# A recommender kernel: an empty GpSimd instruction between row gathers, and the schedule rebuilt around it

## The chip, the cores and the metric

The kernel runs on one core of one Trainium2 chip. A core has five engines [...]: TensorE (PE in the profile, with its weight loads shown apart as PEld), VectorE (DVE), ScalarE (ACT), GpSimd (POOL) and SyncE (SP). Sixteen DMA engines move data between the large memory and the on-chip memory.

The metric is device time in microseconds (us), the median of several executions. These executions are timed without the profiler. The profile is taken of one more execution of the same program, with the profiler on. For this kernel the two differ a lot, and the difference matters for all that follows.

## The reference, cut to what matters

For each of 16384 rows of the batch, the reference averages 32 rows of a table of 50000 x 300 numbers, averages 20 rows from each of three small tables, takes one row from each of four more, and sends the joined 748 features through three layers. A "wide" term, a sum of one number per index, is added before the sigmoid.

```
tok = word_emb[token_idx].mean(axis=1)          # 32 rows of 300
e1 = emb_mh1[mh1_idx].mean(axis=1)              # 20 rows of 64, table of 1000
e2 = emb_mh2[mh2_idx].mean(axis=1)              # ... 5000
e3 = emb_mh3[mh3_idx].mean(axis=1)              # ... 10000
o1..o4 = emb_oh1[oh1_idx], ...                  # one row of 64 each
emb = concatenate([tok, e1, e2, e3, o1, o2, o3, o4], axis=1)    # 748 wide
wide = wide_mh1[mh1_idx].sum(...) + ... + wide_oh4[oh4_idx]
h = relu(emb @ W1 + b1)                         # 748 -> 1024
h = relu(h @ W2 + b2)                           # 1024 -> 512
h = relu(h @ W3 + b3)                           # 512 -> 256
return sigmoid(h @ Wd + bd + wide)              # 256 -> 1
```

All of it is in float32.

## The kernel before

The batch is worked on in 128 tiles of 128 rows. For every tile there are four streams of work.

1. The token rows. GpSimd issues 32 indirect DMAs for a tile; each fetches one row of 300 floats into each of the 128 partitions. Two gathers fill one buffer (a group), there are 6 buffers, and VectorE adds the rows up three groups later. This is 4096 gathers in all.

```
TOK_GROUP = 2
TOK_LAG = 3
tokp = ctx.enter_context(tc.tile_pool(name="tok", bufs=2 * TOK_LAG))

def add_up(t, q, rows):
    a, b = rows[:, 0:TOK_D], rows[:, TOK_D : 2 * TOK_D]
    if q == 0:
        nc.vector.tensor_add(tok_sum, a, b)
    else:
        nc.vector.tensor_add(tok_sum, tok_sum, a)
        to = features[t][:, 0:TOK_D] if q == n_groups - 1 else tok_sum
        nc.vector.tensor_add(to, tok_sum, b)

def tokens(t, it):
    for q in range(n_groups):
        rows = tokp.tile([P, TOK_GROUP * TOK_D], F32, name="tok_rows")
        for r in range(TOK_GROUP):
            j = q * TOK_GROUP + r
            nc.gpsimd.indirect_dma_start(
                out=rows[:, r * TOK_D : (r + 1) * TOK_D],
                out_offset=None,
                in_=word,
                in_offset=bass.IndirectOffsetOnAxis(ap=it[:, j : j + 1], axis=0),
            )
        under_way.append((t, q, rows))
        if len(under_way) > TOK_LAG:
            add_up(*under_way.pop(0))
        yield 1
```

2. The small tables. They stay on chip, each number split into three bf16 parts (`terms`). VectorE makes one-hot rows, TensorE multiplies pairs of them to counts (`pc`), ScalarE writes the counts as fp8 (`cnt`), and in the next tile TensorE multiplies the counts by the tables (`pg`, 138 matmuls for a tile). A tile is cut into 11 steps (`STEPS`), and one step makes the counts of 6 rows in each half of the tile.

3. The layers. Four tiles make a block of 512 rows. Its features are transposed by TensorE, chunk by chunk, and go through the layers as float32 matmuls that are 512 wide. These matmuls are woven between the steps of the next block's tiles.

```
def transposed(x, gs):
    n = len(gs) * P
    for k in range(NK):
        kk = chunk_k[k]
        pt = ps_h.tile([P, BLOCK], F32, name="pt", tag="ph")
        for s, g in enumerate(gs):
            nc.tensor.transpose(pt[:kk, s * P : (s + 1) * P], chunk(g, k), ident)
        nc.vector.tensor_scalar(
            x[:kk, k, 0:n], pt[:kk, 0:n], scale[:kk, k : k + 1], None, ALU.mult
        )
        yield CHUNK_WORK
# ... layer(): for each of n_out outputs, one matmul for each input chunk, then a Relu on ScalarE
```

4. The conversion of the tables to `terms`, once, at the start. VectorE takes the remainders after each bf16 part.

```
for c in range(3):
    ...
    if c:
        nc.vector.scalar_tensor_tensor(
            rows, rows, 2.0 if c == 1 else 1.0, term[c - 1], op0=ALU.mult, op1=ALU.subtract
        )
    nc.scalar.activation(term[c], rows, AF.Copy, scale=2.0 if c == 0 else 1.0)
```

The order in which the instructions of a step are written is the order in which each engine runs them (the schedule is manual). In one step these follow each other: the next one-hots, the counts, one piece of the table conversion, the share of the tile's token groups, the share of the sums over the small tables, and the share of the layers.

```
for i in range(STEPS):
    ...
    hot = one_hots(sc, s, i + 1)
    counts(cnt, hot_now, i)
    tables_on_chip.to(TABLE_PACE * (t * STEPS + i - 2))
    toks.to(n_groups * (i + 1) / STEPS)
    done = next(sums) if sums else 0
    if layers:
        share = (n_h + layers_time) * (i + 1) / STEPS - done
        layers.to((layers_before + share) / LAYER_TIME)
```

Of the kernel before, what the change touches and what calls it, by code (L numbers as in the profile page):

```python
# [17 lines left out]
P = 128  # L18
# [5 lines left out]
TOK_LAG = 3  # L24
BLOCK = 512
HALF = P // 2
N_SMALL = 3 * N_MH + 4
ONEHOT = 6
STEPS = -(-HALF // ONEHOT)
CHUNK_WORK = 1  # L30
TABLE_PACE = 1.2
LAYER_TIME = 10
# [6 lines left out]
G_COLS = TOK_D + 7 * ROW  # L39
# [7 lines left out]
def kernel(  # L47
# [23 lines left out]
    NSUB = BLOCK // P  # L71
# [5 lines left out]
    for f in SMALL:  # L77
# [4 lines left out]
    tokp = ctx.enter_context(tc.tile_pool(name="tok", bufs=2 * TOK_LAG))  # L82
    const = ctx.enter_context(tc.tile_pool(name="const", bufs=1))
    idxp = ctx.enter_context(tc.tile_pool(name="idx", bufs=2))
# [4 lines left out]
    gp = ctx.enter_context(tc.tile_pool(name="g", bufs=NSUB + 1))  # L89
    wp = ctx.enter_context(tc.tile_pool(name="wide", bufs=2 * NSUB))  # L90
    xp = ctx.enter_context(tc.tile_pool(name="x", bufs=1))
# [8 lines left out]
        [(0, 128)],  # L100
        [(128, 256)],
        [(256, 300), (684, 748)],
        [(300, 428)],
        [(428, 556)],
        [(556, 684)],
    ]
# [7 lines left out]
    scale = const.tile([P, NK], F32, name="scale")  # L114
    nc.vector.memset(scale, 1.0)
    nc.vector.memset(scale[:, 0:2], 1.0 / N_TOK)
    nc.vector.memset(scale[0 : TOK_D - 256, 2:3], 1.0 / N_TOK)
    nc.vector.memset(scale[:, 3:4], 1.0 / N_MH)
    nc.vector.memset(scale[0:EMB, 4:5], 1.0 / N_MH)
# [23 lines left out]
    PART = n_h // 6  # L143

    def load_tables(part0, tag):
        raw = xp.tile([P, PART, ROW], F32, name="raw", tag=tag)
# [14 lines left out]
    def convert_tables():  # L161


        tags = ("even", "odd")
        raws = [load_tables(k * PART, tags[k]) for k in range(2)]
        yield
        for part in range(n_h // PART):
            rows = raws[part]
            if 1 <= part < n_h // PART - 1:
                raws.append(load_tables((part + 1) * PART, tags[(part + 1) % 2]))  # L170
            for c in range(3):
                term = [
                    terms[:, part * PART : (part + 1) * PART, k * ROW : (k + 1) * ROW]
                    for k in range(3)
                ]
                if c:
                    nc.vector.scalar_tensor_tensor(
                        rows, rows, 2.0 if c == 1 else 1.0, term[c - 1], op0=ALU.mult, op1=ALU.subtract
                    )
                nc.scalar.activation(term[c], rows, AF.Copy, scale=2.0 if c == 0 else 1.0)  # L180
                yield 1
# [22 lines left out]
    under_way = []  # L204
    features = {}

    def add_up(t, q, rows):

        a, b = rows[:, 0:TOK_D], rows[:, TOK_D : 2 * TOK_D]
        if q == 0:  # L210
            nc.vector.tensor_add(tok_sum, a, b)  # L211
        else:
            nc.vector.tensor_add(tok_sum, tok_sum, a)  # L213
            to = features[t][:, 0:TOK_D] if q == n_groups - 1 else tok_sum
            nc.vector.tensor_add(to, tok_sum, b)  # L215

    def tokens(t, it):


        for q in range(n_groups):  # L220
            rows = tokp.tile([P, TOK_GROUP * TOK_D], F32, name="tok_rows")
            for r in range(TOK_GROUP):
                j = q * TOK_GROUP + r
                nc.gpsimd.indirect_dma_start(  # L224
                    out=rows[:, r * TOK_D : (r + 1) * TOK_D],
                    out_offset=None,
                    in_=word,
                    in_offset=bass.IndirectOffsetOnAxis(ap=it[:, j : j + 1], axis=0),
                )
            under_way.append((t, q, rows))  # L230
            if len(under_way) > TOK_LAG:
                add_up(*under_way.pop(0))
            yield 1

    def last_tokens():
        for group in under_way:
            add_up(*group)

    def load_indices(blk):
# [15 lines left out]
        return it, ix  # L255
# [71 lines left out]
    def small_sums(g, cnt):  # L327
# [3 lines left out]
        for i in (0, 2, 4, 6):  # L331
# [9 lines left out]
            at = TOK_D + i * ROW  # L341
# [9 lines left out]
    def wide_term(g):  # L351
        wide = wp.tile([P, 1], F32, name="wide")
        at = TOK_D + EMB
        nc.vector.tensor_reduce(
            wide,
            g[:, at : at + 6 * ROW].rearrange("p (c d) -> p c d", d=2 * ROW)[:, :, 0:2],
# [3 lines left out]
        nc.vector.tensor_add(wide, wide, g[:, G_COLS - 1 : G_COLS])  # L360
        return wide

    def chunk(g, k):
        if k < 2:
            return g[:, k * P : (k + 1) * P]
        if k == 2:
            return g[:, 2 * P : TOK_D + EMB]
        at = TOK_D + (1 + 2 * (k - 3)) * ROW + 1
        return g[:, at : at + 2 * EMB]

    def transposed(x, gs):

        n = len(gs) * P
        for k in range(NK):
            kk = chunk_k[k]
            pt = ps_h.tile([P, BLOCK], F32, name="pt", tag="ph")
            for s, g in enumerate(gs):
                nc.tensor.transpose(pt[:kk, s * P : (s + 1) * P], chunk(g, k), ident)  # L378
            nc.vector.tensor_scalar(  # L379
                x[:kk, k, 0:n], pt[:kk, 0:n], scale[:kk, k : k + 1], None, ALU.mult  # L380
            )
            yield CHUNK_WORK

    def layer(dst, weights, bias, src, kks, n_out, n):
# [180 lines left out]
```

## Time and profile before

| | us |
|---|---|
| timed executions, without the profiler | 7128.85, 7092.46, 7119.63 |
| their median | 7119.63 |
| the profiled execution | 5271.1 |
| its span in the trace | 5269.3 |

The profiled execution is 1848.5 us shorter than the median of the timed ones. The views of the profile show the profiled execution only.

| engine, profiled execution | busy us | share of the span | instructions |
|---|---|---|---|
| PE | 5094.7 | 97% | 41320 |
| DVE | 3768.8 | 72% | 8014 |
| ACT | 2447.1 | 46% | 1938 |
| POOL | 3897.3 | 74% | 4103 |

How to read the views: a group is a set of instructions of one source line, with its engine, what it writes and reads, the count behind the x, the busy time in us and the mean of one in ns, and after the second bar the idle time of the engine just before these instructions with the name of what ended most of the wait. "issue" means that the engine waited for nothing that the profile shows. In a timeline the columns are the start and the duration in us, the engine, the line, the operation, and in square brackets the idle time before it with its releaser. The ends of matmuls are modelled, so PE's share is not a share of its peak.

### The profile page before, as it was taken

How to read it: one execution, taken by the hardware profiler on the slowest of the kernel's cores; microseconds unless marked ns; L12 is line 12 of the kernel's file. 1: busy time of each engine (PE TensorE's matmuls, PEld its weight loads, DVE VectorE, ACT ScalarE, POOL GpSimd, SP SyncE). 2: the span in 40 equal slices, each digit the busy share in tenths (PEclk: the TensorE clock that was granted, in tenths of full speed). 3: DMA queues.
4: the chain of work that ended last, by engine and by line, in shares of the span. 5: the costliest groups of instructions: out<-in, count | busy, mean ns of one | idle time of the engine just before them, and what ended most of it. 6: DMA issues, size and time to landing. Idle time of an engine off the chain costs nothing.

```text
span 5269.3 us, 104252 instructions
## 1 busy us (share of the span) xinstructions
PE 5094.7 (97%) x41320; PEld 3164.7 (60%) x41320; DVE 3768.8 (72%) x8014; ACT 2447.1 (46%) x1938; POOL 3897.3 (74%) x4103
## 2 busy tenths in 40 slices
PE   4799999999999999999999999999999999999999
PEld 3565656566565656656655656556566566656658
DVE  8777777777777777777777777777777777777752
ACT  5444444444444444444444444444444444444432
POOL 7777777777777777777777777777777777777762
PEclk8899999999999999999999999999999999999999
DMA  6444444444444444444444444444444444444431
GB/s 190 125 125 124 125 125 126 126 125 124 125 125 125 125 124 125 125 125 126 125 124 125 126 125 126 124 125 125 125 125 125 124 126 125 125 125 125 124 103 34
DMA packets 252890, 652.60 MB, mean 124 GB/s; under 512 B 119009, under 2 KB 119524, under 8 KB 252399
## 3 DMA queue, kind: packets, MB, share of 16 engines
q0 software_dynamic: 196608, 629.41, 43.5%
q1 hardware_dynamic: 55791, 16.53, 1.4%
q8 instruction: 323, 5.29, 0.4%
q14 instruction: 168, 1.38, 0.1%
HBM read 645.59 MB, written 0.07 MB: 123 GB/s over the span
## 4 chain that ended last, share of the span: by engine, by line
PE 37%; DMA 23%; DVE 16%; issue 14%; POOL 10%; ACT 0%; DVEq 0%; SPq 0%; POOLq 0%; ACTq 0%
DMA tok_rows<-in_word_emb_dram,it 22%; PE ph L388 20%; PE pg L337 12%; POOL tok_rows L224 10%; DVE own L215 5%; PE pc L312 4%; DVE own L213 3%; DVE slice L294 3%; DVE row L294 2%; DVE x L379 1%; DVE g L343 1%; PE po L413 1%; DVE own L211 0%; DVE g L215 0%; PE po L417 0%
## 5 line engine op out<-in xcount | busy, mean ns | idle before, releaser
L224 POOL DMA_INDIRECT tok_rows<-in_word_emb_dram,it x4096 | 3896.4, 951 | 1293.4 <-issue 755.5
L319 ACT ACTIVATE cnt<-pc 128x1656 fp8e3<-128x1656 f32 (+1 forms) x1408 | 2121.7, 1507 | 2056.4 <-PE pc L312 2026.0
L337 PE MATMUL pg<-terms,cnt 128*128 128x195 bf16 x17664 | 1849.6, 254 | 87.7 <-DVE g L343 86.3
L337 PEld LDWEIGHTS <-cnt 128*128 128x128 fp8e3 x17664 | 1601.3, 144 | 234.6 <-issue 81.1
L388 PE MATMUL ph<-x,w_sb 128*128 128x512 f32 (+5 forms) x3264 | 1474.1, 581 | 4.2 <-DVE x L379 3.5
L215 DVE TENSOR_TENSOR own<-own,tok_rows 128x300 f32<-128x300 f32 x1792 | 857.7, 479 | 680.6 <-DMA tok_rows<-in_word_emb_dram,it 647.3
L388 PE MATMUL ph<-h,w_sb 128*128 128x512 f32 (+2 forms) x2720 | 1211.0, 573 | 0.0
L213 DVE TENSOR_TENSOR own<-own,tok_rows 128x300 f32<-128x300 f32 x1920 | 918.8, 479 | 387.6 <-DMA tok_rows<-in_word_emb_dram,it 335.8
L312 PEld LDWEIGHTS <-row 64*128 64x128 bf16 x16384 | 501.7, 95 | 1041.3 <-DVE own L215 246.1
L294 DVE TENSOR_TENSOR row<-own,sc 128x768 bf16<-128x768 bf16 (+1 forms) x1408 | 762.4, 541 | 162.8 <-PE pc L312 89.5
L312 PE MATMUL pc<-slice,row 64*128 64x138 bf16 x16384 | 758.4, 224 | 70.6 <-DVE slice L294 36.7
L388 PEld LDWEIGHTS ph<-x,w_sb 128*128 128x128 f32 (+1 forms) x3264 | 564.3, 194 | 414.6 <-issue 401.9
L294 DVE TENSOR_TENSOR slice<-own,sc 128x828 bf16<-128x828 bf16 (+1 forms) x1408 | 797.9, 567 | 0.0
L388 PEld LDWEIGHTS ph<-h,w_sb 128*128 128x128 f32 x2720 | 463.3, 192 | 317.9 <-issue 316.0
L397 ACT ACTIVATE h<-ph,b_sb 128x512 f32<-128x512 f32 (+2 forms) x476 | 316.3, 665 | 683.2 <-PE ph L388 678.2
L343 DVE TENSOR_REDUCE g<-pg 128x130 f32<-128x390 f32 (+1 forms) x512 | 259.2, 506 | 151.1 <-PE pg L337 150.8
L379 DVE TENSOR_SCALAR x<-pt,scale 128x512 f32<-128x512 f32 (+4 forms) x204 | 137.0, 712 | 3.7 <-PE pt L378 2.9
L378 PE MATMUL pt<-ident,g 128*128 128x128 f32 (+1 forms) x768 | 104.1, 275 | 3.0 <-DVE x L379 2.5
L211 DVE TENSOR_TENSOR own<-tok_rows 128x300 f32<-128x300 f32 x128 | 61.4, 480 | 49.5 <-DMA tok_rows<-in_word_emb_dram,it 47.3
L378 PEld LDWEIGHTS pt<-ident,g 128*128 128x128 f32 (+1 forms) x768 | 85.5, 141 | 7.7 <-DVE x L379 6.7
L215 DVE TENSOR_TENSOR g<-own,tok_rows 128x300 f32<-128x300 f32 x128 | 60.2, 471 | 22.3 <-DMA tok_rows<-in_word_emb_dram,it 18.3
L413 PE MATMUL po<-h,wd_sb 128*1 128x512 f32 (+2 forms) x136 | 60.9, 566 | 0.3
(34 smaller groups left out, 290.1 us busy)
## 6 DMA issues: line engine op xcount, KB each, us to landing
tok_rows<-in_word_emb_dram,it POOLq DMA_INDIRECT x4096
ix<-in_idx_dram SPq DMA_DIRECT2D x128, 32.0 KB
w_sb<-in_W_dram SPq DMA_DIRECT2D x6, 512.0 KB
raw<-in_mh_dram SPq DMA_DIRECT2D x3, 747.5 KB
it<-in_idx_dram SPq DMA_DIRECT2D x32, 64.0 KB
w_sb<-in_W_dram SPq DMA_DIRECT2D x1, 2048.0 KB
raw<-in_mh_dram SPq DMA_DIRECT2D x1, 617.5 KB
out_dram<-h SPq DMA_DIRECT2D x31, 2.0 KB
```

The lines of the kernel that those rows point to most:

```text
L213: nc.vector.tensor_add(tok_sum, tok_sum, a)
L215: nc.vector.tensor_add(to, tok_sum, b)
L224: nc.gpsimd.indirect_dma_start(out=rows[:, r * TOK_D : (r + 1) * TOK_D], out_offset=None, in_=word, in_offset=bass.IndirectOffsetOnAxis(ap ...
L294: nc.vector.tensor_tensor(one[:, 0:rows, :].rearrange("p i (n d) -> p i n d", d=2), iota[:, 0:n].rearrange("p (n d) -> p n d", d=2).unsque ...
L312: nc.tensor.matmul(pc[:, f, k // n, at : at + n_h], hot[0][half, k, :], hot[1][half, k, :], start=True, stop=True,)
L319: nc.scalar.activation(cnt[:, :, b : b + rows, :].rearrange("l f (g k) h -> l f g (k h)", g=2), pc[:, :, :, 0 : n * n_h], AF.Copy, scale=0 ...
L337: nc.tensor.matmul(pg[:, j, :], by_slice[:, :, h], terms[:, h, :], start=(h == h0), stop=(h == h1 - 1))
L343: nc.vector.tensor_reduce(g[:, at : at + n * ROW].rearrange("p (f d) -> p f d", f=n), pg[:, 0:n, :].rearrange("p f (c d) -> p f d c", c=3) ...
L378: nc.tensor.transpose(pt[:kk, s * P : (s + 1) * P], chunk(g, k), ident)
L379: nc.vector.tensor_scalar(x[:kk, k, 0:n], pt[:kk, 0:n], scale[:kk, k : k + 1], None, ALU.mult)
L388: nc.tensor.matmul(ph[:, 0:n], weights[:kk, k, m * P : (m + 1) * P], src[:kk, k, 0:n], start=(k == 0), stop=(k == len(kks) - 1),)
L397: nc.scalar.activation(dst[:, m, 0:n], ph[:, 0:n], AF.Relu, bias=bias[:, m : m + 1])
```

## The change

The change has these parts.

- An empty GpSimd instruction, `engine_nop`, follows every gather. It computes nothing and nobody waits for it.
- The token groups are no longer tied to their tile. One generator runs over all 1024 groups, and is paced over 704 + 16 steps (`WAKE`), so that the gathers drift behind the counts by up to 16 steps. There are 8 buffers in place of 6, and the sums of a tile's tokens get a tile of their own (`g_tok`).
- The transposes are made tile by tile, the small tables' features and the tokens' apart, each as soon as it is there. The order of the chunks is changed so that the small features come first. The wide term is a 65th column that is transposed along, and is added by VectorE behind the last layer, in place of a matmul for each tile.
- A block of the layers is two tiles (256 rows) in place of four.
- The remainders of the table conversion are made by TensorE, in PSUM: the identity times the rows, minus one half times the terms so far. VectorE has no part in it any more. The pieces are smaller (7 of the 138 slices at once in place of 23).

It is meant to let the gathers follow each other faster, and to keep the other engines from waiting for one another once they do.

```diff
+TOK_BUFS = 8
+WAKE = 16
+LAYER_TILES = 2
+SPLIT = 7
+PART = 3 * SPLIT
-LAYER_TIME = 10
+LAYER_TIME = 2.5
...
-    def tokens(t, it):
-        for q in range(n_groups):
-            rows = tokp.tile([P, TOK_GROUP * TOK_D], F32, name="tok_rows")
-            for r in range(TOK_GROUP):
...
+    def tokens():
+        under_way = []
+        for n in range(n_all):
+            if n < n_all - TOK_LAG:
+                t, q = divmod(n, n_groups)
+                it = token_indices[t // NSUB][:, t % NSUB, :].bitcast(U32)
+                rows = tokp.tile([P, TOK_GROUP * TOK_D], F32, name="tok_rows")
+                for r in range(TOK_GROUP):
+                    j = q * TOK_GROUP + r
+                    nc.gpsimd.indirect_dma_start(
+                        out=rows[:, r * TOK_D : (r + 1) * TOK_D],
+                        out_offset=None,
+                        in_=word,
+                        in_offset=bass.IndirectOffsetOnAxis(ap=it[:, j : j + 1], axis=0),
+                    )
+                    nc.gpsimd.engine_nop()
+                under_way.append((t, q, rows))
+            if n >= TOK_LAG:
                 add_up(*under_way.pop(0))
             yield 1
...
-                if c:
-                    nc.vector.scalar_tensor_tensor(
-                        rows, rows, 2.0 if c == 1 else 1.0, term[c - 1], op0=ALU.mult, op1=ALU.subtract
-                    )
-                nc.scalar.activation(term[c], rows, AF.Copy, scale=2.0 if c == 0 else 1.0)
...
+            left = ps_h.tile([P, SPLIT, ROW], F32, name="left", tag="ph")[:, 0 : b - a, :]
+            nc.tensor.matmul(left, ident, rows(p), start=True, stop=False)
+            for k in range(c):
+                nc.tensor.matmul(left, minus_half, term(p, k), start=False, stop=(k == c - 1))
+            nc.scalar.activation(term(p, c), left, AF.Copy, scale=2.0)
...
+        def add_small(self, t, g):
+            at = self.columns(t)
+            pt = ps_h.tile([P, 4, P], F32, name="pt", tag="ph")
+            nc.tensor.transpose(pt[:, 3, :], g[:, 0:P], ident)
+            for k in range(3):
+                c = (1 + 2 * k) * ROW + 1
+                nc.tensor.transpose(pt[:, k, :], g[:, c : c + P], ident)
+            ...                                        # scaled copies to x_small, one row to wide_row
+        def add_tokens(self, t, g):
+            ...                                        # three transposes, scaled copies to x_tok, x_small
...
+    n_steps = tiles * STEPS + WAKE
...
+        if waiting and step >= waiting[0][0]:
+            block = transpose(*waiting.pop(0)[1:])
+            if block:
+                if layers:
+                    layers.finish()
+                layers = Paced(mlp(block), LAYER_TIME * block.n / P)
+                ...
+        toks.to(n_all * (step + 1) / n_steps)
...
         if layers:
-            layers_before += layers_time
...
+            layers.to(mlp_work * layers.size * (step + 1 - begin) / left + ahead)
```

## The prediction

> **What bounds the kernel now.** I read the times first, then the page's table of engines, the timeline of GpSimd at the start, the groups, and the timeline of TensorE near the end, where the last blocks are narrower.
>
> The times disagree with the trace: 7119.63 us as the median of the timed executions, 5271.1 us for the profiled one. The trace therefore shows the kernel's work, but not what makes it last 7120 us. The first question is which engine can hide 1848 us.
>
> ```profile
> PE 5094.7 (97%) x41320; PEld 3164.7 (60%) x41320; DVE 3768.8 (72%) x8014; ACT 2447.1 (46%) x1938; POOL 3897.3 (74%) x4103
> ...
> L224 POOL DMA_INDIRECT tok_rows<-in_word_emb_dram,it x4096 | 3896.4, 951 | 1293.4 <-issue 755.5
> ...
> L215 DVE TENSOR_TENSOR own<-own,tok_rows 128x300 f32<-128x300 f32 x1792 | 857.7, 479 | 680.6 <-DMA tok_rows<-in_word_emb_dram,it 647.3
> ...
> L213 DVE TENSOR_TENSOR own<-own,tok_rows 128x300 f32<-128x300 f32 x1920 | 918.8, 479 | 387.6 <-DMA tok_rows<-in_word_emb_dram,it 335.8
> ```
>
> PE looks like the bound, but its share is of modelled ends. VectorE's largest waits are for the gathers' transfers (647 and 336 us), and GpSimd itself waits mostly for "issue", that is for nothing. The timeline of GpSimd shows this from the first gather on, before the other engines have anything to hold it back with:
>
> ```profile
> 3.12 1.10 POOL L224 DMA_INDIRECT tok_rows<-in_word_emb_dram,it  x1 [1.65 <-DMA it<-in_idx_dram]
> 4.53 0.95 POOL L224 DMA_INDIRECT tok_rows<-in_word_emb_dram,it  x1 [0.30 <-issue]
> 5.78 0.95 POOL L224 DMA_INDIRECT tok_rows<-in_word_emb_dram,it  x1 [0.30 <-issue]
> 7.04 0.95 POOL L224 DMA_INDIRECT tok_rows<-in_word_emb_dram,it  x1 [0.30 <-issue]
> ...
> 22.07 1.50 POOL L224 DMA_INDIRECT tok_rows<-in_word_emb_dram,it  x1 [0.30 <-issue]
> ...
> 25.16 2.09 POOL L224 DMA_INDIRECT tok_rows<-in_word_emb_dram,it  x1 [0.30 <-issue]
> ...
> 5190.39 0.94 POOL L224 DMA_INDIRECT tok_rows<-in_word_emb_dram,it  x1 [0.30 <-issue]
> ```
>
> The reader is to see the start-to-start distance: 1.253 us, with 0.95 us in the gather and 0.30 us behind it. Over the whole timeline 4039 of the 4095 distances lie between 1.2 and 1.3 us. So 4096 x 1.253 = 5132 us, out of the 5187 us from the first gather to the last. The missing 57 us are the few longer distances: 43 of them after 5000 us, where the buffers come free late, and 11 in the first 130 us. Behind the last gather come 79 us of tail. The profiled execution is bound by GpSimd, one gather after the other.
>
> PE is a close second. I worked out its floor from distances in the same trace[...].
>
> ```profile
> 5134.80 0.54 PE L312 MATMUL pc<-slice,row 64*128 64x138 bf16 x12
> 5135.27 0.39 PE L337 MATMUL pg<-terms,cnt 128*128 128x195 bf16 x2
> 5135.50 4.48 PE L388 MATMUL ph<-h,w_sb 128*128 128x512 f32 x10
> 5139.91 0.42 PE L312 MATMUL pc<-slice,row 64*128 64x138 bf16 x8
> ...
> 5198.06 4.51 PE L388 MATMUL ph<-h,w_sb 128*128 128x256 f32 x20
> 5202.50 0.42 PE L312 MATMUL pc<-slice,row 64*128 64x138 bf16 x8
> ```
>
> Ten passes of 512 columns take 4.41 us (5135.50 to 5139.91), twenty passes of 256 take 4.44 us. Twelve count matmuls take 0.47 us, and fifteen small-table matmuls 1.36 us (5112.95 to 5114.31 in the same view). A block of four tiles has 180 layer passes, since float32 is recorded as two. For a tile: counts 128 x 0.04 = 5.1; small tables 138 x 0.0907 = 12.5; layers 180 x 0.441 / 4 = 19.8; transposes and the wide term about 1.0. That is 38.4 us, and 128 tiles make 4920 us, 4% below the gathers' 5132.
>
> For the timed executions nothing else has room for 1848 us. PE would have to be slower by more than a third, against a granted clock of 0.989 in the trace. If the gathers set the pace there as well, one takes (7119.6 - 79) / 4096 = 1.72 us, 0.47 us more than under the profiler. This is an inference: no view shows a timed execution.
>
> [...] the DMA engines are busy only four tenths of the time. [...] the gathers of 1.50 and 2.09 us above coincide with the table remainders (1.72 us at 21.03 and 1.71 us at 24.72). [...]
>
> **The change, part by part.**
>
> The empty instruction: 4096 of them on GpSimd. [...] the change puts something between them without the profiler. I take it that this has the same effect, and that a gather with its empty instruction then takes what it takes in the trace, 1.253 us. Removed from the path: 4096 x (1.72 - 1.253) = 1913 us. If the empty instruction added 0.05 us behind each gather, 205 us would come back; I see 0.30 us of pause already in each distance and count nothing.
>
> The drift is a hint of the same number. The gathers are spread over 720 steps and the counts over 704. That only makes sense where the gathers are slower by about 2% than the rest. With the rest at 4920 us plus 1 to 2% of stalls, the gathers would be near 5100 to 5150, and 5132 fits.
>
> More buffers and the drift: the 57 us of long distances shrink, mostly the 43 at the end. VectorE's adds in program order no longer wait as often. I count 40 us gained.
>
> Layers in blocks of two: 180 passes of 0.222 for two tiles make 20.0 us for a tile in place of 19.8, 17 us in all on PE, and PE has slack. The extra Relu instructions go to ScalarE, which is busy 46%.
>
> Transposes tile by tile: seven for a tile in place of six, but no more wide matmuls (256 in all); even on PE. On VectorE five smaller copies for a tile replace six of 0.74 us for four tiles; some 1.5 us more for a tile, 200 us on an engine with 1500 us idle, off the path.
>
> Tables by TensorE: 12 VectorE instructions of 1.71 us go, and with them some 10 us of delayed gathers in the first 130 us. The PE has room there.
>
> The tail: behind the last gather there remain the landing and the adds (about 4 us), the transposes and copies (about 2), one tile's layers of 180 passes of 0.11 us (96 passes take 10.8 us at the end of the trace, so 20 us), the sigmoid and the store (about 3): near 30 us in place of 79.
>
> Sum: first gather at 3, 4096 gathers at 1.253 = 5132, long distances 20, tail 30: 5185 us. I add 15 us for the uncertain cost of the empty instruction and predict 5200 us, a saving of 1920 us or 27%.
>
> **The rivals.**
>
> First: the empty instruction does nothing, and a gather stays at 1.72 us. For it: no view shows the cause of the 0.47 us, and if the profiler speeds up the gathers by something else (another path of dispatch, a slower neighbour), an instruction more is only a cost. Then the rest of the change brings the tail, 50 us, and loses up to 200: 7070 to 7320 us. Against it: the whole rest of the change only pays once the gathers are quick.
>
> Second: the gathers become quicker than in the trace[...]. Then PE is the bound: 4920, plus about 90 us at the start while there is nothing for the layers to do yet, plus 20 of tail and 1% of stalls: about 5080 us. For it: the 0.30 us pause has no cause in the trace.
>
> Third: the empty instruction works in part or has a price, 1.3 to 1.4 us for a gather: 5375 to 5785 us.
>
> Fourth: the time before has to do with PE's clock outside the profile, not with gathers. Then the change, which leaves PE's work as it is, would leave 7100 us. The granted clock speaks against it.
>
> **Range and chances.** I give the main path about 60%, the second rival 15, the third 13, and the two without a gain 12. The main path and the second rival span 5050 to 5290; part of the third has to be in the range. So 5050 to 5480. Faster by over 2% in 0.88, within 2% in 0.06, slower in 0.06.
>
> **What would show the steps right or wrong.** The timed executions should come to within 3% of the profiled one. In the trace of the changed kernel GpSimd's distances should stay at 1.25 us or a little more, from 3 us to about 5160 us, with hardly a long one, and the rest behind the last gather should be near 30 us. PE's pairs at 256 columns should be 0.222 us apart. If the timed executions stay above 7000 us while the trace shows 5200, the step "the empty instruction does what the profiler does" is wrong; if the trace shows distances above 1.4 us, its price is wrong; if PE runs without a gap and GpSimd waits for VectorE, the second rival is right.

## Result: slower by 7.5%

| | before | after |
|---|---|---|
| median of the timed executions, us | 7120.24 | 7651.85 |
| lowest to highest | 7092.46 to 7128.85 | 7636.04 to 7655.15 |
| ratio after/before | | 1.0749, 95% interval 1.0716 to 1.0783 |
| span of the profiled execution, us | 5269.3 | 7633.9 |
| its mean granted TensorE clock | 0.989 | 0.874 |

Predicted were 5200 us, in a range of 5050 to 5480. The changed kernel's profiled execution is as long as its timed ones. That makes the 5269 us trace of the kernel before, on which the prediction stood, the one to be doubted; experiment 1 tests it.

### The profile after

The page of the changed kernel: engines with busy time and share, the granted clock in 40 slices (tenths of full speed), the chain that ended last, and the groups.

```profile
PE 5989.8 (78%) x46912; PEld 4706.2 (62%) x46912; DVE 3890.9 (51%) x8502; ACT 2577.7 (34%) x2445; POOL 3878.3 (51%) x4103
...
PEclk8888888888888898888898988888888888888889
...
PE 52%; another core or an unknown queue 19%; DVE 13%; issue 11%; ACT 5%; DVEq 0%; SPq 0%; DMA 0%; ACTq 0%
...
L255 POOL DMA_INDIRECT tok_rows<-in_word_emb_dram,it x4096 | 3877.4, 947 | 3715.7 <-DVE own L242 2425.8
L348 ACT ACTIVATE cnt<-pc 128x1656 fp8e3<-128x1656 f32 (+1 forms) x1408 | 2123.8, 1508 | 3203.6 <-remote 1658.8
L366 PE MATMUL pg<-terms,cnt 128*128 128x195 bf16 x17664 | 2179.9, 273 | 428.2 <-issue 380.1
...
L323 DVE TENSOR_TENSOR row<-own,sc 128x768 bf16<-128x768 bf16 (+1 forms) x1408 | 763.0, 542 | 1848.7 <-remote 1374.1
```

No engine is the bound: PE falls from 97% to 78%. GpSimd's gathers are as short as before (947 ns against 951), but it now waits 2426 us for VectorE to free a buffer. VectorE and ScalarE in turn wait for "remote", and 19% of the chain is "another core or an unknown queue". There is one core only. The words mean that the view found no instruction whose end lies close before the end of the wait. Both waiting instructions, the counts' copy and the next one-hots, wait for TensorE's count matmuls.

The timeline of GpSimd answers to the one shown of the kernel before (start, duration, engine, instruction, idle time before it with its releaser):

```profile
3.09 1.10 POOL L255 DMA_INDIRECT tok_rows<-in_word_emb_dram,it  x1 [1.62 <-DMA it<-in_idx_dram]
4.49 0.95 POOL L255 DMA_INDIRECT tok_rows<-in_word_emb_dram,it  x1 [0.30 <-issue]
...
24.61 0.95 POOL L255 DMA_INDIRECT tok_rows<-in_word_emb_dram,it  x1 [0.30 <-issue]
25.86 0.94 POOL L255 DMA_INDIRECT tok_rows<-in_word_emb_dram,it  x1 [0.30 <-issue]
27.11 0.95 POOL L255 DMA_INDIRECT tok_rows<-in_word_emb_dram,it  x1 [0.30 <-issue]
33.66 0.94 POOL L255 DMA_INDIRECT tok_rows<-in_word_emb_dram,it  x1 [5.61 <-DVE own L242]
...
7593.56 0.94 POOL L255 DMA_INDIRECT tok_rows<-in_word_emb_dram,it  x1 [0.30 <-issue]
```

The distance is 1.25 us with the 0.30 us pause, as before, and the two stretched gathers near 22 and 25 us are gone. 81% of all distances are still below 1.3 us. What makes the time is the others, such as the 5.61 us at 33.66.

What happens in such a wait, in the timeline of all engines in the middle of the changed kernel:

```profile
2988.50 1.48 PE L443 MATMUL ph<-h,w_sb 128*128 128x256 f32 x6
...
2993.59 0.54 PE L341 MATMUL pc<-slice,row 64*128 64x138 bf16 x12
...
2994.50 0.29 PE L366 MATMUL pg<-terms,cnt 128*128 128x195 bf16 x1 [0.36 <-issue]
2994.93 0.94 POOL L255 DMA_INDIRECT tok_rows<-in_word_emb_dram,it  x1 [0.31 <-DVE g_tok L242]
...
2995.91 0.33 PE L366 MATMUL pg<-terms,cnt 128*128 128x195 bf16 x2 [1.12 <-issue]
...
2996.17 0.95 POOL L255 DMA_INDIRECT tok_rows<-in_word_emb_dram,it  x1 [0.30 <-issue]
...
2997.42 0.95 POOL L255 DMA_INDIRECT tok_rows<-in_word_emb_dram,it  x1 [0.30 <-issue]
...
2998.68 0.95 POOL L255 DMA_INDIRECT tok_rows<-in_word_emb_dram,it  x1 [0.30 <-issue]
2998.75 0.32 PE L366 MATMUL pg<-terms,cnt 128*128 128x195 bf16 x1 [0.88 <-issue]
...
3001.59 1.03 PE L366 MATMUL pg<-terms,cnt 128*128 128x195 bf16 x5 [0.39 <-issue]
3001.78 1.55 ACT L348 ACTIVATE cnt<-pc 128x1656 fp8e3<-128x1656 f32 x1 [8.55 <-remote]
3001.78 0.56 DVE L323 TENSOR_TENSOR row<-own,sc 128x768 bf16<-128x768 bf16 x1 [7.01 <-remote]
...
3002.42 2.81 PE L443 MATMUL ph<-h,w_sb 128*128 128x256 f32 x6
...
3003.62 0.94 POOL L255 DMA_INDIRECT tok_rows<-in_word_emb_dram,it  x1 [4.00 <-DVE own L236]
```

The twelve count matmuls end by 2994.13. ScalarE and VectorE, both idle from 2994.8 on at the latest, go on 7.6 us after that end, at the same moment. The trace's semaphore events agree: the one semaphore for which both wait rises at 3001.76. The ends of matmuls are modelled, so the trace can't tell a late signal from a matmul that ended late; "late signal" stands for both from here on. Between, TensorE gets through its small-table matmuls at one or two in 0.7 us, with "issue" before each, where it otherwise needs 0.09 us for one. Gathers run one after the other until 2998.68. When they have stopped for lack of a buffer (none starts between 2998.68 and 3003.62), the signal arrives and TensorE's pauses end. Its clock, however, had fallen to half at 2996.68 and stays there until 3006.92: the six layer matmuls at 3002.42 take 2.81 us, those at 2988.50 took 1.48.

### The profile page after: what moved, and what is told of

Its sections match the earlier page's. It is cut to its first block, busy times and chain, and to the rows that moved or that the text cites. A ratio compares the mean times of both kernels' runs of the same rounds, so it can differ in the third digit from the quotient of the medians.

```text
span 7633.9 us, 120613 instructions
## 1 busy us (share of the span) xinstructions
PE 5989.8 (78%) x46912; PEld 4706.2 (62%) x46912; DVE 3890.9 (51%) x8502; ACT 2577.7 (34%) x2445; POOL 3878.3 (51%) x4103
## 3 DMA queue, kind: packets, MB, share of 16 engines
q0 software_dynamic: 196608, 629.41, 30.0%
## 4 chain that ended last, share of the span: by engine, by line
PE 52%; another core or an unknown queue 19%; DVE 13%; issue 11%; ACT 5%; DVEq 0%; SPq 0%; DMA 0%; ACTq 0%
PE ph L443 23%; PE pg L366 17%; PE pc L341 8%; ACT cnt L348 4%; DVE own L238 4%; DVE slice L323 3%; DVE own L242 3%; PE po L468 1%; DVE row L323 1%; ACT h L452 1%; PE pt L411 1%; PE pt L427 1%; PE left L193 0%; DVE g L372 0%
## 5 line engine op out<-in xcount | busy, mean ns | idle before, releaser
L366 PE MATMUL pg<-terms,cnt 128*128 128x195 bf16 x17664 | 2179.9, 273 | 428.2 <-issue 380.1
L366 PEld LDWEIGHTS <-cnt 128*128 128x128 fp8e3 x17664 | 1808.8, 147 | 702.8 <-issue 586.8
L443 PE MATMUL ph<-h,w_sb 128*128 128x256 f32 (+1 forms) x5200 | 1381.4, 408 | 80.5 <-issue 76.9
L443 PE MATMUL ph<-x_small,w_sb 128*128 128x256 f32 (+3 forms) x4160 | 1203.0, 418 | 78.0 <-issue 58.4
L443 PEld LDWEIGHTS ph<-h,w_sb 128*128 128x128 f32 x5200 | 1010.5, 208 | 253.2 <-issue 129.3
L452 ACT ACTIVATE h<-ph,b_sb 128x256 f32<-128x256 f32 (+1 forms) x910 | 427.5, 470 | 1762.0 <-remote 779.9
L443 PEld LDWEIGHTS ph<-x_small,w_sb 128*128 128x128 f32 (+1 forms) x4160 | 827.4, 213 | 223.3 <-issue 104.6
L443 PE MATMUL ph<-x_tok,w_sb 128*128 128x256 f32 (+1 forms) x2080 | 619.9, 405 | 20.4 <-issue 20.2
L443 PEld LDWEIGHTS ph<-x_tok,w_sb 128*128 128x128 f32 x2080 | 408.7, 208 | 86.0 <-issue 34.5
L468 PE MATMUL po<-h,wd_sb 128*1 128x256 f32 (+1 forms) x260 | 86.9, 458 | 46.2 <-ACT h L452 41.3
```

The costliest lines, as they stand in the source:

```text
L366: nc.tensor.matmul(pg[:, j, :], by_slice[:, :, h], terms[:, h, :], start=(h == h0), stop=(h == h1 - 1))
L443: nc.tensor.matmul(ph[:, 0:n], weights[: src.shape[0], k, m * P : (m + 1) * P], src, start=(k == 0), stop=(k == len(srcs) - 1),)
L452: nc.scalar.activation(dst[:, m, 0:n], ph[:, 0:n], AF.Relu, bias=bias[:, m : m + 1])
L468: nc.tensor.matmul(po[:, 0:n], wd_sb[:, k : k + 1], h3[:, k, 0:n], start=(k == 0), stop=(k == M3 - 1))
```

## Experiments

All times are medians in us; "ratio" is to runs of the kernel before on the same chip, with its 95% interval. The chips fall into two kinds: on some the kernel before takes 7120 to 7140 us (chips 3, 5, 11 and 13, and the first result), on others 5261 to 5265 (9 and 12). What the expectations call slow and quick kinds of chip are these two. Letters in the expectations name theories; each text says what its theory holds. Each of the six chips was used in one sitting only, in which all executions of the kernel before lie within 0.6% of each other. So the kind may be a property of the chip or of the sitting; "kind of chip" stands for either.

**1. The kernel before, unaltered.** No edit.

> The kernel before, unchanged, profiled and timed once more. Theory A (timed executions of it are slow because bursts of gathers hold back TensorE's signals, and the profiled one happened to escape that): timed again near 7120 us; if this profile shows the same regime as the timed ones, its span is near 7100 us, TensorE's granted clock is well under 0.99, and ScalarE starts its copy of the counts several us after the last count matmul, as in the changed kernel. Theory B (the profiler itself makes the gathers of this kernel quicker): the span is again near 5270 us and ScalarE is never more than 0.12 us late.

Measured: 7132.73, ratio 1.0002 (0.9988 to 1.0017); the profiled execution spans 7119.1 us. The profiler does not make the kernel quick. Its page:

```profile
PE 5689.1 (80%) x41320; PEld 3498.5 (49%) x41320; DVE 3799.8 (53%) x8014; ACT 2468.4 (35%) x1938; POOL 3892.8 (55%) x4103
...
PEclk8789998899889898989889899998998888898999
...
L224 POOL DMA_INDIRECT tok_rows<-in_word_emb_dram,it x4096 | 3891.9, 950 | 3147.7 <-DVE own L215 1661.2
L319 ACT ACTIVATE cnt<-pc 128x1656 fp8e3<-128x1656 f32 (+1 forms) x1408 | 2123.9, 1508 | 3919.4 <-remote 2198.8
...
L294 DVE TENSOR_TENSOR row<-own,sc 128x768 bf16<-128x768 bf16 (+1 forms) x1408 | 762.7, 542 | 2005.1 <-remote 1439.3
```

The same signature, without the change. In the 5269 us trace the copy's line was this one, with the matmuls themselves as the releaser:

```profile
L319 ACT ACTIVATE cnt<-pc 128x1656 fp8e3<-128x1656 f32 (+1 forms) x1408 | 2121.7, 1507 | 2056.4 <-PE pc L312 2026.0
```

I worked out from the traces by how much each copy starts after both its last count matmul and the copy engine's previous instruction have ended, and how many gathers started in the 5 us before that end. In the 5269 us trace, all but some 40 of the 1408 steps have four gathers there, and no copy is over 0.12 us late. In this 7119 us trace: two gathers or fewer, 444 steps, one of them over 0.5 us late (by 1.0); three, 446 steps, 46% late; four, 518 steps, 86% late, by 3.4 us on average. A gather itself is the same on both: median distance 1.25 us, last data 2.5 us after its start. The packets of the DMA queue q8, which the page names "instruction", take no longer either: 323 in each trace, of 0.98 us in the median in the 5269 us trace and 0.99 in this one.

**2. The empty instruction alone.** Taken from the changed kernel, and put into the kernel before.

```diff
-                    nc.gpsimd.engine_nop()      # e2: the changed kernel without it
+                nc.gpsimd.engine_nop()          # e3: the kernel before with it
```

> The changed kernel without the empty GpSimd instructions, all else as it is. Theory A (bursts of gathers do the harm, the empty instruction changes little): 7500 to 7700 us, within 2% of the changed kernel's 7652. Theory C (the empty instruction is what costs, some 0.13 us for each of 4096 gathers): 7100 us or less. The prediction's theory, that it is what makes gathers quick, would have it slower than 7652.

> The kernel before with an empty GpSimd instruction after each gather and nothing else. The prediction's theory: about 5270 us. Theory A: near 7120 us, within 2%. Theory C (the empty instruction costs): 7500 to 7650 us.

Measured: without it 7667.74, ratio 1.0751 (1.0720 to 1.0782), where the first result of the changed kernel was 1.0749. The changed kernel's ratio is 1.088 to 1.091 in other sittings (experiment 8), so this pair would not show an effect of one per cent. With it in the kernel before 7226.95, ratio 1.0132 (1.0093 to 1.0172). The gathers' distance stays at 1.25 us in both. It brings nothing, and costs 1.3% in the second pair.

**3. No gathers.** The adds work on one constant buffer; the token sums are left out.

```diff
-            rows = tokp.tile([P, TOK_GROUP * TOK_D], F32, name="tok_rows")
-            for r in range(TOK_GROUP):
-                ...gather...
+            rows = still          # e4: in the kernel before; e9: in the changed one
```

> The kernel before without the 4096 gathers: VectorE adds the same constant buffer as often as before, all other work is unchanged. Theory A (gathers in close succession hold back the signals that TensorE gives when its matmuls are done): 4950 to 5150 us, ScalarE never more than 0.2 us late after the last count matmul, granted clock over 0.97. Rival D (VectorE's adds or TensorE's own load are what delays TensorE): 6500 to 7100 us.

> The changed kernel without its gathers and empty instructions; VectorE adds a constant buffer as often as before. On any chip 4980 to 5120 us by theory A or F: without gathers nothing holds TensorE back, and TensorE's own work of some 4920 us is the bound. If TensorE is held back by something else on the slow kind of chip: over 6000 us there.

Measured: the kernel before 5150.39 (ratio 0.9783, 0.9763 to 0.9802, on a chip where it takes 5265); the changed kernel 5185.86 (ratio 0.7264, 0.7235 to 0.7293, on one where the kernel before takes 7139). The second, from its page:

```profile
PE 5112.1 (99%) x46912; PEld 4175.1 (81%) x46912; DVE 3890.7 (75%) x8503; ACT 2600.8 (50%) x2445; POOL 0.9 (0%) x7
...
PEclk9999999999999999999999999999999999999999
...
L341 ACT ACTIVATE cnt<-pc 128x1656 fp8e3<-128x1656 f32 (+1 forms) x1408 | 2124.6, 1509 | 1608.8 <-PE pc L334 1607.3
```

The same chip on which the changed kernel takes 7765 us runs all its other work at full clock, with no "remote". Without gathers the new layout takes 36 us more than the old one (the two ran on different chips), and 66 us more than the 5120 expected at most. All the rest of the loss needs the gathers.

**4. The same bytes by another way.** In the kernel before, each pair of gathers becomes one plain load of 256 consecutive rows, issued by SyncE. The rows are not those of the indices.

```diff
-            for r in range(TOK_GROUP):
-                ...gather...
+            at = (t * n_groups + q) % 192 * 256
+            nc.sync.dma_start(
+                out=rows, in_=word[at : at + 256, :].rearrange("(p r) d -> p (r d)", r=TOK_GROUP)
+            )
```

> The kernel before with each pair of gathers replaced by one plain load of the same number of bytes, issued by SyncE (other rows than the indexed ones are added up). Slow kind of chip: 5000 to 5300 us if the harm comes from gathers as such[...]; 6500 us or more if the bytes that arrive in the on-chip memory do it. Quick kind: 5000 to 5250 us.

Measured: 5161.17, ratio 0.7235 (0.7214 to 0.7255), on a chip where the kernel before takes 7133.

```profile
PE 5062.0 (98%) x41320; PEld 3146.7 (61%) x41320; DVE 3794.7 (74%) x8014; ACT 2444.0 (47%) x1938; POOL 0.9 (0%) x7
...
L315 ACT ACTIVATE cnt<-pc 128x1656 fp8e3<-128x1656 f32 (+1 forms) x1408 | 2119.6, 1505 | 1947.8 <-PE pc L308 1947.7
```

629 MB land in the same buffers and VectorE makes the same adds, and no signal is late. It is neither the bytes nor VectorE nor TensorE's own load, but the gathers, as GpSimd issues them. Which part of a gather, GpSimd's issue of it or its scattered rows, was not taken apart. The number of packets does not explain it: the traces have 196608 for all gathers and 294912 for the loads.

**5. Half the bytes.** Gathers of 150 numbers. The table is seen as 100000 half rows, and the unchanged indices pick among these, so that the numbers are others.

```diff
+    half_rows = word.rearrange("v (t d) -> (v t) d", t=2)
...
-                    out=rows[:, r * TOK_D : (r + 1) * TOK_D],
+                    out=rows[:, r * TOK_D : r * TOK_D + TOK_D // 2],
...
-                    in_=word,
+                    in_=half_rows,
```

> The kernel before with gathers of 150 floats in place of 300 (the second half of each row is left out; the adds read the first half twice). [...] If the bytes moved hold TensorE back: 5200 to 6300 us. If it is the number of gathers[...]: 7000 to 7150 us.

Measured: 5263.18, ratio 0.9997 (0.9988 to 1.0007), on a chip where the kernel before takes 5265. There the gathers' pace does not depend on their bytes. The question asked, whether the bytes hold TensorE back, needs the other kind of chip, and this run does not answer it.

**6. A real pause between gathers.** A memset after each gather of the kernel before (e5, f3, h1), and in place of the empty instruction in the changed one (g2).

```diff
+    filler = const.tile([P, 256], F32, name="filler")     # h1: [P, 384]
...
+                nc.gpsimd.memset(filler, 0.0)             # after each gather
```

> The kernel before with a GpSimd memset of 128 x 256 floats after each gather, so that gathers cannot start less than about 1.55 us apart. Theory A with the threshold that the traces show (with at most two gathers in the last 5 us TensorE's signals were never late, with four of them late in 86% of the cases): fewer than a fifth of the steps late and 6400 to 6900 us, faster than before although GpSimd does more. Theory E (the number of gathers counts, not their distance): 7100 us or more.

> The kernel before with a GpSimd memset of 128 x 256 floats after each gather, which on the quick kind of chip set the gathers 1.46 us apart and gave 6066 us. Slow kind of chip: 6300 to 6900 us, faster than the kernel before although GpSimd has more to do, if closeness of gathers is what holds TensorE back (theory A); 7100 to 7400 us if only their number counts. Quick kind: 6066 us again.

> The changed kernel with a memset of 128x256 on GpSimd between gathers in place of the empty instruction, so gathers start about 1.44 us apart and not 1.25. On a chip where the kernel before takes about 7130: theory F expects 6700 to 7200, well under the changed kernel, since fewer gathers fall on each TensorE signal; whether it comes under the 6770 of the kernel before with the same memset tells whether the layout costs anything once gathers are thinner. If the empty instruction already did what a pause does, it would be no faster than the changed kernel. On a chip where the kernel before takes 5265: 4096 x 1.44 = 5898 and a tail, 5900 to 6080.

> The kernel before with a memset of 128x384 on GpSimd after each gather. With the memset of 128x256 a gather started every 1.44 us; 128 elements more should add about 0.11 us (one memset took 0.33 us with 256 elements and 0.10 us with one), so about 1.56 us, and the gathers alone would need 4096 x 1.56 = 6390 us and a tail of some 80: 6470. On a chip where the kernel before takes about 7130: theory F (fewer gathers in a TensorE signal's way, fewer late signals) expects 6500 to 6760, below the 6770 with the shorter memset, and less idle time of ScalarE's count copies with no local releaser. If the gain of the memset came from something that its length does not touch, it would be 6770 or more. On a chip where the kernel before takes 5265: 6470 to 6500.

| kernel, memset | chip: before takes, us | time, us | ratio (95%) |
|---|---|---|---|
| before, 256 (e5) | 5265 | 6065.68 | 1.1523 (1.1504 to 1.1542) |
| before, 256 (f3) | 7133 | 6770.14 | 0.9494 (0.9472 to 0.9515) |
| changed, 256 (g2) | 7140 | 7010.93 | 0.9816 (0.9787 to 0.9845) |
| before, 384 (h1) | 5261 | 6501.91 | 1.2356 (1.2336 to 1.2377) |

The gathers of the kernel before with the memset, on the chip of the slower kind (f3):

```profile
3000.59 0.95 POOL L225 DMA_INDIRECT tok_rows<-in_word_emb_dram,it  x1 [0.17 <-issue]
3001.54 0.33 POOL L231 MEMSET filler<- 128x256 f32 x1
3002.04 0.95 POOL L225 DMA_INDIRECT tok_rows<-in_word_emb_dram,it  x1 [0.17 <-issue]
...
3004.43 0.33 POOL L231 MEMSET filler<- 128x256 f32 x1
3006.89 0.95 POOL L225 DMA_INDIRECT tok_rows<-in_word_emb_dram,it  x1 [2.13 <-DVE own L216]
```

They start 1.45 us apart. Spread out like this, they cost 15% where the kernel is bound by them and gain 5% where TensorE suffers from them; the changed kernel gains 9.8% on itself (7011 against 7772 on that chip). The mechanism held only in part, though: fewer than a fifth of the steps were expected to be late. With the memset 52% of the steps with three gathers in 5 us are late and 74% of those with four, so as many copies are late as before (670 of 1408, and 650 in e1). With four gathers they are less late (1.9 us in place of 3.4, over all such steps), with three they are later (1.5 in place of 1.0); all lateness together falls from 2209 to 1866 us, and TensorE's pauses from 1624 to 1334 us (estimates, see the table below). The run with 384 was to show whether a longer pause gains more; it fell on a chip where the kernel before takes 5261 us, so it shows a price only, and that question stays open. Neither version beats the kernel before on both kinds of chip.

**7. Narrow layer matmuls.** In the kernel before, each matmul of 512 columns as two of 256: into one PSUM tile with one Relu (e7, e10), and each with its own tile and Relu (e11).

```diff
-            for k, kk in enumerate(kks):
-                nc.tensor.matmul(ph[:, 0:n], ..., src[:kk, k, 0:n], ...)
+            for at in range(0, n, 256):
+                part = slice(at, min(at + 256, n))
+                for k, kk in enumerate(kks):
+                    nc.tensor.matmul(ph[:, part], ..., src[:kk, k, part], ...)
```

> The kernel before with every layer matmul of 512 columns split into two of 256, as many TensorE instructions more as the changed kernel has (about 5600 matmuls), and nothing else changed. If the changed kernel is slower because its blocks of two tiles need more TensorE instructions: 7550 to 7700 us. If it is slower for another part of the change: 7120 to 7200 us.

> The kernel before with each layer matmul of 512 columns split into two of 256, in one PSUM tile and with one Relu for both; 5267 us on the quick kind of chip. On the slow kind: 7550 to 7700 us if the number of TensorE instructions makes the changed kernel slower there; 7100 to 7200 us if not. On the quick kind: 5267 us again.

> As the run before, but each half of 256 columns has its own PSUM tile and its own Relu, so that TensorE hands over twice as often and after half the time (952 Relus in place of 476). On the slow kind of chip 7400 to 7700 us if what costs is that TensorE waits for late signals more often with half the slack; about the same as the run before if not. On the quick kind: 5265 to 5320 us.

Measured: on a chip where the kernel before takes 5265, 5267.10, ratio 1.0004 (0.9995 to 1.0013). On one where it takes 7139: 7369.61, ratio 1.0317 (1.0283 to 1.0351), and with the split groups 7365.00, ratio 1.0323 (1.0288 to 1.0358). So the narrower matmul costs nothing by its columns, and 3.2% where TensorE is late. That lies between the two expected ranges (7100 to 7200 and 7550 to 7700): the narrow matmuls are a part of the loss and not the whole. Why they cost anything there, no run shows. More hand-overs (910 Relus in the trace, in place of 476) add nothing to it.

**8. The changed kernel on other chips, and without the drift.** e8, f1 and g1 are the changed kernel, unaltered; f2 has 6 buffers, and its gathers are paced over the tiles' own steps.

```diff
-TOK_BUFS = 8
+TOK_BUFS = 6
...
-        toks.to(n_all * (step + 1) / n_steps)
+        toks.to(n_all * (step + 1) / (tiles * STEPS))
```

> The changed kernel, unchanged, beside the kernel before. The kernel before took 7128 us on one chip and 5265 us on another. Theory F (on some chips TensorE's signals are held back while gathers run, and the ratio of 1.075 belongs to those): where the kernel before takes 5265 us, this one takes 5100 to 5250 us, as predicted; where the kernel before takes about 7125 us, 7600 to 7700 us. Theory G (the change is slower by itself): over 5300 us even where the kernel before takes 5265.

> The changed kernel once more, unchanged. If the kernel before takes about 5265 us on this chip: 5100 to 5250 us by theory F (the prediction's sum was right for such chips), over 5300 us by theory G (slower by itself). If the kernel before takes about 7130 us: 7640 to 7780 us again.

> The changed kernel again, unaltered, to have it once beside a run of the kernel before of 5265 us. If the kernel before takes about 5265 us here: theory F (the harm comes only from TensorE's late signals, which that kind of chip does not have) expects 5100 to 5250, because the gathers then set the pace again at 4096 x 1.253 = 5132 us and fewer buffers run out; theory G (the new layout costs time by itself, in hand-overs or narrower matmuls) expects more than 5300. If the kernel before takes about 7130 us here: 7640 to 7780, a ratio of 1.075 to 1.092, and nothing new.

> The changed kernel with six token buffers in place of eight and the gathers paced over the 1408 steps of the counts, without the 16 more: the drift undone, all else kept. Slow kind of chip, if longer bursts of gathers are what the change adds to the harm: 7350 to 7500 us; if not: 7650 to 7780. Quick kind of chip: 10 to 80 us more than the changed kernel.

Measured for the changed kernel: 7764.98, 7777.21 and 7772.26, ratios 1.0884, 1.0912 and 1.0880, each within 0.4% either way. Without the drift 7697.50, ratio 1.0796 (1.0760 to 1.0831), on the chip of the second. Drift and two more buffers, meant to help, cost about 1%; this is in the range expected if longer bursts of gathers are not what the change adds. These three chips, and those of the first result and of experiment 2, were of the kind on which the kernel before takes over 7100 us. What the change does on the other kind was not seen. An estimate: without gathers it takes 5186 us, so with them it can hardly gain more than 1.5% on 5265.

### Where TensorE's time goes

Estimates from the traces, good to some 3%: distances between the starts of TensorE's matmuls, split into what their columns need at full rate (0.84 ns for a column in float32, from 429 ns for 512 columns and 215 for 256 in the 5269 us trace; half of that in bf16, from 56 ns for 128 columns where float32 takes 109), pauses (over 0.35 us too long), and the rest. The rest is some 400 us even where the clock is hardly ever halved; what it has beyond that goes with the time at half clock. In us:

| trace | at full rate | pauses | rest | time at half clock |
|---|---|---|---|---|
| before, 5269 us | 4674 | 195 | 391 | 120 |
| before, 7119 us (e1) | 4674 | 1624 | 812 | 1427 |
| before, narrow layers, 7375 us (e10) | 4674 | 1765 | 926 | 1775 |
| after, 7634 us | 4679 | 1911 | 1035 | 1929 |
| after without gathers, 5185 us (e9) | 4679 | 81 | 416 | 18 |

TensorE's work is the same in all. The change adds 287 us of pauses and 223 us of rest to e1. The clock belongs to the second sum, which grows with the time at half clock. The traces with more pauses have the lower clock: its mean is 0.998 without gathers (e9), 0.900 in e1, 0.874 after, and 0.934 in h1, where TensorE merely waits for slow gathers. In the trace of the changed kernel the clock falls to half 313 times; in the 3 us before such a fall TensorE is busy for 31% in the median, in the 3 us before these for 79%, and in the 3 us before the clock rises again for 100%. What sets the clock was not tried alone. The stretch shown above has the same order:

```profile
2988.00:2993.00 5.00, 5.00 (x47) 4.32 (x46) 3.48 (x8) 2.13 (x2) 3.78 (x5) 1.00 0.42 107
2994.00:2996.60 2.60, 0.76 (x9) 0.42 (x3) 0.74 (x2) 0.00 (x0) 1.99 (x3) 1.00 0.47 127
2996.70:3001.50 4.80, 2.03 (x7) 0.77 (x7) 0.00 (x0) 0.00 (x0) 2.31 (x3) 0.50 0.45 120
```

The columns are the stretch and its length, the busy time of PE, PEld, DVE, ACT and POOL (with the number of instructions), the granted clock, and the share and GB/s of the DMA engines. TensorE is busy for 0.76 of the 2.60 us from 2994.00 on while the clock is still full; only then is it halved. The low clock follows the pauses; about 60% of the pauses in e1 begin while the clock is full.

## Why the prediction was wrong, by its own steps

- **The step that failed** is the inference behind "the first question is which engine can hide 1848 us": that the timed executions are bound by gathers of 1.72 us, and that the profiler makes them 1.253. A profiled execution of the kernel before takes 7119 us as well, with gathers 1.25 us apart, and GpSimd waits for buffers (experiment 1). What the runs show in its place: TensorE is held up while gathers run, with 1624 us of pauses in that trace, and the kernel takes 5161 us on the same kind of chip once plain loads take the gathers' place (experiment 4). The two first times fit the two kinds of chip; on which chips they were taken is not known. That an empty instruction does what the profiler does was an assumption of the author's that no trace showed. So "removed from the path: 4096 x (1.72 - 1.253) = 1913 us" had nothing to remove, and the empty instruction measured -0.2 to +1.3% (experiment 2).
- **"PE would have to be slower by more than a third, against a granted clock of 0.989"**: it is. In e1 its full-rate work of 4674 us takes 7110. The clock quoted against it, and against the fourth rival, came from the other kind of chip, and the clock shows only the smaller part of the loss. That rival named the engine rightly, though not the cause, and left 7100 us where it became 7652: with TensorE the one that suffers, its new shape was not neutral. The first rival was right that the empty instruction does nothing, and missed with 7070 to 7320 us because it kept the gathers of 1.72 us as the bound.
- **"And PE has slack"**: true by columns (passes of 256 columns are 0.216 us apart in the changed kernel, in the median, where 0.222 was expected; experiment 7: +2 us where 17 were counted, on the quick kind of chip). On the other kind the same edit costs 231 us, the largest part of the loss that was isolated.
- **TensorE's floor of 4920 us** was 4.5% short: without gathers the kernel before takes 5150. So even on the quick kind of chip all work on its gathers can save at most 115 us of 5265. With start, tail and stalls added, the sum of the second rival, 5080 us, was 1.4% short.
- **More buffers and the drift, 40 us gained**: they cost about 1% (experiment 8). The hint read from 720 steps against 704 was a slip besides, as are the 704 steps and 1024 groups named with the change: 128 tiles of 11 steps are 1408, so the 16 are 1.1%, and 4096 gathers in pairs are 2048 groups.
- **Tables by TensorE**: the stretched gathers are gone, as expected. Why the table remainders coincide with stretched gathers was not shown. Not every VectorE instruction stretches the gather beside it: the adds of token rows, 0.48 us each, run beside gathers all the time, and the mean gather of the kernel before stays at 951 ns. The effect of this part on the time was not measured alone.
- **The tail**: 40 us from the last gather at 7593.56 to the end at 7633.9, where 30 were expected and 79 were before: right in kind, and small beside a loss of 532.
- **Timed within 3% of the profiled execution, distances of 1.25 us**: both hold, at 7650 us. "Hardly a long one" does not: 19% of the distances are longer than 1.3 us, and the last gather starts at 7593.56 and not at 5160. The two signs that hold could not tell the theories apart, since the distance between undisturbed gathers was never what set the time of 7120.

Of the 7.5 to 9.1% of loss, the narrow matmuls make 3.2 and drift with buffers about 1, if parts add up, which was not shown. The remaining 3 to 5% lie in parts not tried alone: transposes tile by tile, the new order, the paced layers, the tables by TensorE. The narrow layers were tried in the kernel before, not undone in the changed one. Why gathers hold TensorE back at all, and on one kind of chip only, stays open. With the memset in both, the changed kernel is still 3.6% above the old one (7011 against 6770, on two chips of the same kind).

## What to carry to other kernels

When the profiled execution and the timed ones differ by a third, measure the unaltered kernel again before explaining the gap: it may be the chip or the sitting and not the profiler, and a bound read from one trace may not be the bound where the time was taken. Where several engines wait for "remote" or "issue" on a single core, look for one engine whose signals come late to all, and test it by taking away what runs beside it. While gathers delay TensorE, its shape is not free: matmuls of half the width cost 3.2% and gathers spaced by a memset gained 5%, neither of which full-rate arithmetic shows. Where TensorE is not delayed, the same width cost nothing and the same spacing cost 15%.

## What the hardware showed that was not expected

- Two kinds of chip (or of sitting) differ by 35% on the same program (7130 and 5265 us). Without the gathers the times are close: 5150 us (e4) on the quick kind, 5161 with plain loads (f4) and 5186 for the changed kernel (e9) on the slow one; no single kernel without gathers ran on both. What differs was not found.
- On the slow kind, TensorE runs at one or two matmuls in 0.7 us, and its signals come late, by 7.6 us in the stretch shown, beside gathers 1.25 us apart. Beside plain loads of the same bytes no signal is late, and the kernel takes 5161 us (f4).
- A gather of 128 rows takes GpSimd 1.25 us from start to start. Where the gathers set the time, the kernel takes 5263 us with rows of 150 numbers and 5265 with rows of 300 (e6). With an empty instruction behind each gather the distance is 1.25 us as well (e3, and the changed kernel), with a memset of 0.33 us it is 1.45 (f3).
